# Layer D routed in four chunks of 4, 4, 4 and 3 elements, with places found sooner and indexed rows closer together

## The chip, the cores and the metric

The kernel runs on one core of a Trainium2 chip. The core has five engines that work side by side, each through its own queue in order: TensorE (PE: matrix multiplications, with its weight loads shown as PEld), VectorE (DVE), ScalarE (ACT), GpSimd (POOL) and SyncE (SP, which here only starts transfers). The transfers run on 16 DMA engines. The metric is the device time of one execution in microseconds (us); lower is better.

## The reference

The input is 16 batch elements of 256 tokens with 128 channels, in float32. Four sublayers follow each other, each added to its input after a layer norm: attention a (8 heads, causal, with a term from the geometry of the heads), a mixture of experts, attention b (16 heads, no mask), and the same mixture of experts again with the same weights:

```python
x = x + attn_a(layernorm(x))
x = x + ffn(layernorm(x))
x = x + attn_b(layernorm(x))
x = x + ffn(layernorm(x))

def ffn(tgt):                       # E = 8 experts, F = 512
    logits = einsum('bsd,ed->bse', tgt, Wr) + br
    top_v, top_i = top_k(logits, 2)
    top_w = softmax(top_v)
    router_w = sum(one_hot(top_i, 8) * top_w[..., None], axis=-2)
    h = relu(einsum('bsd,efd->bsef', tgt, W1) + b1)
    o = einsum('bsef,edf->bsed', h, W2) + b2
    return layer_norm(tgt + einsum('bsed,bse->bsd', o, router_w), gamma, beta)
```

Each token uses two of eight experts. What an element needs is its own tokens alone, so elements can be at different sublayers at a time.

## The kernel before

**Work by element and by chunk.** The two attentions run element by element (`attention`), element 0 to 15 of a, then of b. Attention b takes its 16 heads in eight pairs; a pair is scores on PE (tag `s`, L487), row maxima on DVE (L510), then, when all maxima are there, transposed scores (tag `st`, L564), exponentials on ACT, and a weighted sum on PE (L613). The experts run by chunks of elements (`experts`): layer "B" behind attention a, layer "D" behind attention b. `CHUNKS` lists how many elements each chunk has. In D the first five chunks are sorted by expert; the last one, of a single element, is computed with every expert (`every_expert`, called dense), with weights of 0 where a token didn't choose one.

**A sorted chunk.** For each of its elements: a layer norm into the tile `tgt`, its transpose, the router's logits. Then a chain of some 35 small DVE operations with two groups of matmuls between them (`count`, L1005, and `ranks`, L1015 to L1023): the two best experts of each token, each token's rank within its expert, the places of its two rows in the sorted order (`idx`, L1077), and the expert of each tile (`dti`). POOL then writes the rows of `tgt` to those places in memory, 128 rows by one indexed transfer (`scatter`, L1113): two to each 128 tokens, so four to an element. A tile is 128 sorted rows of one expert; since each expert's rows are filled up to whole tiles, a chunk of n elements gets `tiles_of(2n)` = 4n + 7 of them, used or not. Four tiles' rows are read back in one transfer (`rows`) and transposed on PE (`turn_rows`, L1169). Each tile needs its expert's weights (578 KB, SP's queue, ring `we` of six), the first product (`up`, L1182: eight matmul instructions, as each float32 product is two), a ReLU on ACT and DVE, the second product (`down`, L1206, eight more), and a store of four tiles' rows (`os`). When all of a chunk's stores have landed, each element gets its two rows per token back (`gather`, L1271, four indexed transfers on POOL), weighs and adds them on DVE (`part`, L1296) and finishes with the second layer norm (`finish`) and, in D, the write of the output.

**What sets the order.** At build time a planner in Python orders all instructions. Each piece of work is a `Task` with an engine, a planned duration, a `key` (smaller goes first), the tasks that it comes after, and the ring slots (`RINGS`) that it takes and gives back. Keys count pairs of heads: an element of b takes eight, `ends[b]` is its attention's end in this count. The routing chain has the key `key8`, the scatters `key + 0.3`, tile i of a D chunk `key + LATE + PACE_D * i`. While attention still has `st` tasks to place, two `up` tasks are put at least `RATES` apart in planned us (D: 4.1). Indexed transfers are put at least `GAP` = 2.6 planned us apart, and each is made to wait for an ACT instruction that the plan ends between the one transfer (plus 1.3 us) and the next (`apart`). The planned times only set the order within each engine's queue (and these waits); on the chip each engine takes its queue as data comes.

Of the kernel before, what the change touches and what calls it, by code (L numbers as in the profile page):

```python
# [25 lines left out]
NF = F // P  # L26


CHUNKS = {"B": (2, 4, 5, 5), "D": (4, 4, 3, 2, 2, 1)}
CTM = NT * max(max(c) for c in CHUNKS.values())  # L30
TB = 4
NR = 3
# [11 lines left out]

LAT = dict(mem=3.0, qk=6.0, sh=2.4, sc=4.0, rows=4.0, we=4.5, os=5.5, g=5.0)

EARLY = 2.0


WIDE = 6  # L50

RATES = {"B": (4.1, 3.4, 4.1), "D": (4.1,)}


def tiles_of(ct):
# [16 lines left out]
def block_kernel(  # L72
# [20 lines left out]
    NBE = x.shape[0] // T  # L93
    assert all(sum(c) == NBE for c in CHUNKS.values()) and CHUNKS["D"][-1] == 1

# [39 lines left out]
    for b in range(4, 8):  # L135
# [4 lines left out]
    rows_max = [max(  # L140
        tiles_of(NT * n) for c in CHUNKS.values() for k, n in enumerate(c) if k % NX == i
    ) * P for i in range(NX)]
# [80 lines left out]
    def clear_k(i):  # L223
# [11 lines left out]

    RINGS = dict(
        mm=4, att=2, mv=8, lnr=8, nm=6, xn=2, xT2=3, qks=2, mem=3, m=7, ms=2, pT=6, avs=4,
        on=2, oT=2, tgt=14, rl=2, rw=5, didx=5, dti=3, we=6, x4=3, xT=2, hT=3, o4=2,
        r0=NR, r1=NR, y=4, gw=1, ye=1, z=2,
    )  # L240

# [1 line left out]
    GAP = 2.6  # L243
# [118 lines left out]
    all_s, all_st = [], []  # L362

    def attention(kind, b, slot):
# [12 lines left out]
        x = xb[b]  # L377
        ahead = slot - (0.0 if causal else EARLY)
        g = {}
# [344 lines left out]
    order = {"last": None, "xs": {}, "os": {}, "n": 0}  # L724

    def experts(layer, c, ends, need, dense=False):


        n = f"{layer}{c}"
        b0, nb = sum(CHUNKS[layer][:c]), CHUNKS[layer][c]  # L730
        bs = range(b0, b0 + nb)
# [8 lines left out]
        rl_h, tgt_h, t_tgt, t_lg, tT_of = Hold("rl"), {}, {}, [], {}  # L740

        for b in bs:
            key = ends[b] + 0.2
            t0 = (b - b0) * NT

            def tgt_tile(b=b):
                g["tgt", b] = work.tile(
                    [P, NT, C], F32, tag="tgt", name=f"tgt_{n}_{b}", bufs=RINGS["tgt"]
                )
                return g["tgt", b]  # L750
            t_tgt[b], tgt_h[b] = normed(
                lambda b=b: xb[b], f"{n}_{b}", key, [at_x[b]], "tgt", tgt_tile)

            def bias(b=b):

                nc.gpsimd.tensor_tensor(
                    xb[b], xb[b], beta_sb.unsqueeze(1).to_broadcast([P, NT, C]), ALU.add
                )
            at_x[b] = Task("POOL", 0.73, bias, key + 3, [t_tgt[b]])
            t_tT, tT, tT_h = turned(  # L760
                lambda b=b: g["tgt", b], f"{n}_{b}", key, [t_tgt[b]], [tgt_h[b]])
            tT_of[b] = tT, t_tT, tT_h
            mm = Hold("mm")

            def logits(b=b, tT=tT):
                g["lg", b] = ps = ps_mm.tile([P, NT, E], F32, tag="mm", name=f"lg_{n}_{b}")
                for t in range(NT):
                    nc.tensor.matmul(
                        ps[:, t, :], lhsT=tT()[:, t * P:(t + 1) * P], rhs=wr_sb,
                        start=True, stop=True,  # L770
                    )

            def keep_logits(b=b, t0=t0):
                if b == b0:
                    g["rl"] = small.tile([P, ct, E], F32, tag="rl", name=f"rl_{n}",
                                         bufs=RINGS["rl"])
                nc.vector.tensor_tensor(
                    g["rl"][:, t0:t0 + NT, :], g["lg", b],
                    br_sb.unsqueeze(1).to_broadcast([P, NT, E]), ALU.add,
                )  # L780
            e = Task("PE", 0.26, logits, key, [t_tT], take=[mm], use=[tT_h])
            t_lg.append(Task("DVE", 0.1, keep_logits, key, [e] + t_lg[-1:], use=[mm],
                             take=[rl_h] if b == b0 else []))
# [120 lines left out]


        key = max(ends[b] for b in bs) + 0.2
        key8 = key
        k8 = ct * E
        per = 0.14 + 0.0011 * k8
        shape = [P, ct, E]  # L910
# [119 lines left out]
        e = Task("PE", 0.3, count, key8, chain, take=[mm1])  # L1030
        chain = [e]
        dve(0.27, total, use=[mm1])
        e = Task("PE", 0.6, ranks, key8, chain, take=[mm2])
# [77 lines left out]
        def scatter(t, k):  # L1111
            b = b0 + t // NT
            i = apart(nc.gpsimd.indirect_dma_start(  # L1113
                out=x_rows[0:ne * P, :], out_offset=bass.IndirectOffsetOnAxis(
                    ap=g["idx"][:, k, t:t + 1], axis=0),
                in_=g["tgt", b][:, t % NT, :], in_offset=None,
                bounds_check=ne * P - 1, oob_is_err=False,
            ))

            gr = f"sc_{n}"  # L1120
            tc.declare_no_dep(i.ins, group=gr, reason="each row is written once")
            tc.add_to_no_dep_group(gr, i.ins)
        t_sc = []
        free = order["xs"].get(q, []) + zeroed[q]
        for k in range(2):
            for t in range(ct):
                b = b0 + t // NT
                t_sc.append(Task(
                    "POOL", 1.25, lambda t=t, k=k: scatter(t, k), key + 0.3 + 0.01 * len(t_sc),
                    [t_idx[k]] + free, use=[idx_h, tgt_h[b]], kb=64, lat=LAT["sc"] - 1.3,  # L1130
                ))

# [92 lines left out]
        for i in range(ne):  # L1225
            b, j = divmod(i, TB)
            kk = tile_key(i)
            w_h, hT_h, mm1, mm2 = Hold("we"), Hold("hT"), Hold("mm"), Hold("mm")
            if j == 0:
                x4_h, xT_h, mm3, o4_h = Hold("x4"), Hold("xT"), Hold("mm"), Hold("o4")  # L1230
                e = Task("SP", 0.4, lambda b=b: rows(b), kk - 2.5, t_sc, take=[x4_h],
                         kb=256, lat=LAT["rows"])
                t_rows.append(e)
                e = Task("PE", 0.46, lambda b=b: turn_rows(b), kk - 1, [e],
                         take=[mm3, xT_h], use=[x4_h])
                t_xT = Task("ACT", 0.48, lambda b=b: keep_rows(b), kk - 1, [e], use=[mm3])
                t_out = []
            t_load = Task("SP", 0.95 if j == 0 else 0.5, lambda i=i: load(i), kk - 3,
                          [t_ti], take=[w_h], use=[ti_h], kb=592, lat=LAT["we"], order=[t_load])
            t_up_last = t_up = Task("PE", 0.98, lambda i=i: up(i), kk, [t_load, t_xT],  # L1240
                                    take=[mm1, hT_h], use=[w_h, xT_h], order=[t_up_last],
                                    kind="up")
            t_up.rate = RATES[layer][min(c, len(RATES[layer]) - 1)]
            r1 = Task("DVE", 0.27, lambda i=i: relu_v(i), kk, [t_up], use=[mm1, w_h])
            r2 = Task("ACT", 0.76, lambda i=i: relu_s(i), kk, [t_up], use=[mm1, w_h])
            t_dn = Task("PE", 0.98, lambda i=i: down(i), kk, [r1, r2],
                        take=[mm2, o4_h] if j == 0 else [mm2], use=[hT_h, w_h],
                        order=t_dns[-1:])
            t_dns.append(t_dn)
            t_out.append(Task("DVE", 0.2, lambda i=i: keep_out(i), kk, [t_dn], use=[mm2, w_h]))  # L1250
            loads.append(t_load)
            if j == TB - 1 or i == ne - 1:
                stores.append((i, Task(
                    "SP", 0.4, lambda b=b: store(b), kk, t_out + order["os"].get(q, []),
                    use=[o4_h], kb=256, lat=LAT["os"], lag=LAG_OS)))
# [22 lines left out]
        for b in bs:  # L1278
# [3 lines left out]
            for k in range(2):  # L1282
                r_h = Hold(f"r{k}")
                e = [None]
# [52 lines left out]
    ends = {"B": {}, "D": {}}  # L1337
    for kind, b in seq:
        layer = "B" if kind == "a" else "D"
        ends[layer][b] = attention(kind, b, slots[kind, b])  # L1340
        b0 = 0
        for c, k in enumerate(CHUNKS[layer]):
            if b == b0 + k - 1:
                experts(layer, c, ends[layer], slots["b", b0] - NEED if layer == "B" else None,
                        layer == "D" and c == len(CHUNKS[layer]) - 1)
            b0 += k
# [7 lines left out]
    begun = [0.0, 0]  # L1354
    moved = [-GAP]
# [11 lines left out]
    def start(t):  # L1367
        s = max(t.ready + t.lag, free[t.eng])
        if t.eng == "POOL" and t.kb:
            s = max(s, moved[0] + GAP)  # L1370
        if t.kind == "up" and len(all_st) > begun[1]:
            s = max(s, begun[0] + t.rate)
        for h in t.take:
            q, n = rings[h.ring], RINGS[h.ring]
            if len(q) >= n:
                if q[-n].left:
                    return None
                s = max(s, q[-n].done)
            if h.ring == "att" and len(q) > 1:
                if q[-1].left or q[-2].left:  # L1380
                    return None
                s = max(s, q[-1].done, q[-2].done)
        return s
# [34 lines left out]
    while left:  # L1418
        best = None
        for e in ENGS:  # L1420
# [4 lines left out]
            s, t = min(((s, t) for s, t in c if s <= s0), key=lambda st: st[1].key - stay(st[1]))  # L1425
# [3 lines left out]
        s, t, c = best  # L1429
# [94 lines left out]
```

## Time and profile before

The median of three runs is 945.51 us (942.85 to 948.49). The profiled execution took 950.31 us; its span, from the first to the last instruction, is 948.6 us at a mean granted TensorE clock of 0.978.

How the chunks of layer D lie in that span, in us from its start (the element's end is the add at L718; places are the two `idx` casts; the others are starts of the first and last instruction):

| chunk | elements | tiles | last element's end | places | scatters | up-matmuls | gathers |
|---|---|---|---|---|---|---|---|
| 0 | 0-3 | 23 | 441.6 | 470, 471 | 491-531 | 550.2-653.7 | 666-744 |
| 1 | 4-7 | 23 | 577.0 | 608, 611 | 610-650 | 663.4-770.8 | 794-839 |
| 2 | 8-10 | 19 | 677.5 | 706, 708 | 708-739 | 775.4-843.1 | 863-889 |
| 3 | 11, 12 | 15 | 751.7 | 775, 775 | 776-793 | 845.8-877.4 | 892-910 |
| 4 | 13, 14 | 15 | 812.1 | 841, 844 | 842-860 | 878.7-908.9 | 922-939 |
| dense | 15 | - | 851.4 | - | - | 910-934 | - |

The table shows three stretches: attention b with the tiles of B beside it (to 547), attention b with the tiles of D beside it, and from about 850 a tail of tiles alone, closed by the dense element. Element 11 ends at 720.8.

| engine | busy us | share of the span |
|---|---|---|
| DMA, queue of SP (163.69 MB) | | 58.4% of 16 engines |
| DMA, queue of POOL (16.27 MB) | | 5.5% of 16 engines |
| L510 DVE maxima x128 | 155.8 | 16% |
| L1182 PE up, layer D x760 | 102.4 | 11% |
| L1206 PE down, layer D x760 | 107.1 | 11% |
| L1113 POOL scatters, layer D x60 | 60.1 | 6% |
| L1271 POOL gathers, layer D x60 | 62.8 | 7% |

Matmuls are pipelined, so their busy time is the time in which at least one of the group is under way. A view of a stage gives busy times of all engines in a stretch of the span; the chain of waits follows the work that ended last back from the end.

### The profile page before, as it was taken

The numbers are of one execution on the slowest core, as the hardware profiler recorded it, in microseconds if no ns is written. First come the engines' busy times: TensorE is split into PE (matmuls) and PEld (weight loads), VectorE is DVE, ScalarE is ACT, GpSimd is POOL, SyncE is SP. The second block draws the span as 40 slices with busy tenths as digits, with TensorE's granted clock in tenths as the row PEclk, the third lists the DMA queues.
The fourth block names the chain that finished last, engine by engine and source line by source line (L and its number), as shares of the span: only waits on it lengthen the run. The fifth ranks groups of instructions, "written<-read, shape, count | busy, mean of one in ns | idle before, by whom it ended". The sixth has DMA issues, their size and how long they took to land. (4 is left out here: it accounts for less than half of the span.)

```text
span 948.6 us, 24346 instructions
## 1 busy us (share of the span) xinstructions
PE 889.4 (94%) x8941; PEld 720.4 (76%) x8941; DVE 618.1 (65%) x1919; ACT 512.6 (54%) x1188; POOL 416.9 (44%) x553
## 2 busy tenths in 40 slices
PE   7788899998999999999999999999989999899995
PEld 5555688887887778787777777777767877799985
DVE  4578687778657757456686457745766665564666
ACT  5355565665555664565655555556645655545421
POOL 4134635654653554313554225443534314444633
PEclk9799899999999999999999999999999999999998
DMA  4222667666765587575776767566856675599991
GB/s 128 57 70 73 232 194 208 202 208 194 232 187 186 165 207 183 187 204 176 186 197 192 221 180 202 168 190 208 188 142 192 216 185 166 170 306 348 372 316 36
DMA packets 115191, 181.96 MB, mean 192 GB/s; under 512 B 11904, under 2 KB 79360, under 8 KB 115072
## 3 DMA queue, kind: packets, MB, share of 16 engines
q1 hardware_dynamic: 106704, 163.69, 58.4%
q0 software_dynamic: 7936, 16.27, 5.5%
q8 instruction: 71, 1.16, 0.5%
q10 hardware_dynamic: 432, 0.45, 0.2%
q14 instruction: 48, 0.39, 0.1%
HBM read 145.63 MB, written 34.34 MB: 190 GB/s over the span
## 5 line engine op out<-in xcount | busy, mean ns | idle before, releaser
L510 DVE TENSOR_REDUCE m_b<-s_b 128x4 f32<-128x1024 f32 x128 | 155.8, 1220 | 59.9 <-PE s_b L487 39.5
L252 ACT ACTIVATE pT_b<-st_b 128x1024 f32<-128x1024 f32 x128 | 129.9, 1026 | 68.4 <-PE st_b L564 49.2
L252 ACT ACTIVATE hT_D<-h_D,we_D 128x128 f32<-128x128 f32 (+1 forms) x301 | 89.7, 372 | 103.2 <-issue 34.5
L487 PE MATMUL s_b<-qk 31*128 31x256 f32 x1024 | 134.9, 405 | 4.7 <-DVE m_b L510 3.1
L564 PE MATMUL st_b<-qk 32*128 32x256 f32 x1024 | 131.4, 409 | 3.7 <-issue 1.7
L252 ACT ACTIVATE hT_B<-h_B,we_B 128x128 f32<-128x128 f32 x276 | 81.1, 365 | 75.0 <-DVE hT_B L1189 38.6
L1206 PEld LDWEIGHTS o_D<-we_D,hT_D 128*128 128x128 f32 x760 | 93.6, 192 | 23.6 <-ACT hT_D L252 12.0
L1206 PE MATMUL o_D<-we_D,hT_D 128*128 128x128 f32 x760 | 107.1, 287 | 4.5 <-ACT hT_D L252 2.6
L1206 PE MATMUL o_B<-we_B,hT_B 128*128 128x128 f32 x736 | 106.3, 288 | 3.4 <-ACT hT_B L252 2.8
L1206 PEld LDWEIGHTS o_B<-we_B,hT_B 128*128 128x128 f32 x736 | 90.7, 192 | 24.4 <-ACT hT_B L252 14.2
L1182 PE MATMUL h_D<-xT_D,we_D 128*128 128x128 f32 x760 | 102.4, 282 | 0.1
L1271 POOL DMA_INDIRECT r_B<-os,idx_B x64 | 67.9, 1062 | 75.7 <-DMA we_B<-in_we_dram 21.0
L1182 PE MATMUL h_B<-xT_B,we_B 128*128 128x128 f32 x736 | 100.6, 280 | 0.2 <-ACT xT_B L252 0.2
L1182 PEld LDWEIGHTS h_D<-xT_D,we_D 128*128 128x128 f32 x760 | 92.5, 193 | 9.9 <-issue 7.4
L1113 POOL DMA_INDIRECT xs<-tgt_D,idx_D x60 | 60.1, 1001 | 87.7 <-DVE idx_D L1077 17.9
L1182 PEld LDWEIGHTS h_B<-xT_B,we_B 128*128 128x128 f32 x736 | 89.7, 192 | 10.3 <-issue 8.6
L487 PEld LDWEIGHTS s_b<-qk 31*128 31x128 f32 x1024 | 80.8, 186 | 17.7 <-issue 5.5
L564 PEld LDWEIGHTS st_b<-qk 32*128 32x128 f32 x1024 | 79.1, 188 | 17.2 <-issue 7.2
L1271 POOL DMA_INDIRECT r_D<-os,idx_D x60 | 62.8, 1047 | 62.0 <-ACT hT_D L252 30.4
L1113 POOL DMA_INDIRECT xs<-tgt_B,idx_B x64 | 64.7, 1011 | 50.7 <-ACT hT_B L252 12.8
L500 DVE TENSOR_TENSOR s_a<-s_a,cmask 128x512 f32<-128x512 f32 x64 | 44.6, 697 | 42.7 <-PE s_a L487 22.5
L1189 DVE TENSOR_SCALAR hT_D<-h_D,we_D 128x128 f32<-128x128 f32 x95 | 33.0, 350 | 56.7 <-PE h_D L1182 23.7
(401 smaller groups left out, 1620.0 us busy)
## 6 DMA issues: line engine op xcount, KB each, us to landing
we_D<-in_we_dram SPq DMA_DIRECT2D x103, 578.0 KB
we_B<-in_we_dram SPq DMA_DIRECT2D x92, 578.0 KB
qk<-qkm SPq DMA_DIRECT2D x104, 64.0 KB
x_B<-xs SPq DMA_DIRECT2D x20, 256.0 KB
os<-o_B SPq DMA_DIRECT2D x20, 256.0 KB
x_D<-xs SPq DMA_DIRECT2D x20, 256.0 KB
os<-o_D SPq DMA_DIRECT2D x20, 256.0 KB
qkm<-qks_b SPq DMA_DIRECT2D x16, 256.0 KB
```

Source lines behind the costliest of these rows:

```text
L252: i = getattr(nc.scalar, name)(*args, **kw)
L487: nc.tensor.matmul(ps[:, j, col:col + nk], lhsT=qT[r:r + 31, t * P:(t + 1) * P], rhs=kT[r:r + 31, 0:nk], start=True, stop=True,)
L500: nc.vector.tensor_tensor(dg, dg, cmask.unsqueeze(1).unsqueeze(1).to_broadcast([P, 2, 2, P]), ALU.add,)
L510: nc.vector.tensor_reduce(m[:, :, heads].rearrange("p t j -> p j t"), ps.rearrange("p j (t k) -> p j t k", k=T), axis=AX.X, op=ALU.max, ne ...
L564: nc.tensor.matmul(ps[:, j, col:col + T - q0], lhsT=kT[r:r + 32, t * P:(t + 1) * P], rhs=qT[r:r + 32, q0:T], start=True, stop=True,)
L1113: i = apart(nc.gpsimd.indirect_dma_start(out=x_rows[0:ne * P, :], out_offset=bass.IndirectOffsetOnAxis(ap=g["idx"][:, k, t:t + 1], axis=0) ...
L1182: nc.tensor.matmul(ps[:, f, :], lhsT=w[:, f * P:(f + 1) * P], rhs=g["xT", b][:, j * P:(j + 1) * P], start=True, stop=True,)
L1189: nc.vector.tensor_scalar(g["hT", i][:, f, :], g["h", i][:, f, :], g["w", i][:, W_B1 + f:W_B1 + f + 1], 0.0, ALU.add, ALU.max)
L1206: nc.tensor.matmul(ps, lhsT=g["hT", i][:, f, :], rhs=g["w", i][:, W_2 + f * C:W_2 + (f + 1) * C], start=(f == 0), stop=(f == NF - 1),)
L1271: apart(nc.gpsimd.indirect_dma_start(out=g["r", k, b][:, t, :], out_offset=None, in_=o_rows[0:ne * P, :], in_offset=bass.IndirectOffsetOnAxis(
```

## The change

- Layer D's sorted chunks are 4, 4, 4 and 3 elements, in place of 4, 4, 3, 2 and 2. The dense element stays. Layer B's chunks stay.
- `AHEAD` holds three numbers that are taken off keys: of the elements' layer norms and logits (0), of the routing chain (6, in both layers), and of the scatters (0).
- Two `up` tasks of D are planned 4.1 us apart in the first two chunks and 4.4 in the other two.
- The ring of `tgt` tiles has 18 slots, where it had 14.
- `turn_rows` of one batch of tiles is never put ahead of that of the batch before, across chunks as well.
- Indexed transfers are planned 2.6 us apart as before while more than 24 `st` tasks are still to be placed (three elements of attention b), and 1.4 behind that. With 1.4 no ACT instruction lies between two that follow at that distance, so `apart` names none.

```diff
-CHUNKS = {"B": (2, 4, 5, 5), "D": (4, 4, 3, 2, 2, 1)}
+CHUNKS = {"B": (2, 4, 5, 5), "D": (4, 4, 4, 3, 1)}
...
+AHEAD = 0, 6, 0
...
-RATES = {"B": (4.1, 3.4, 4.1), "D": (4.1,)}
+RATES = {"B": (4.1, 3.4, 4.1), "D": (4.1, 4.1, 4.4, 4.4)}
...
-        on=2, oT=2, tgt=14, rl=2, rw=5, didx=5, dti=3, we=6, x4=3, xT=2, hT=3, o4=2,
+        on=2, oT=2, tgt=18, rl=2, rw=5, didx=5, dti=3, we=6, x4=3, xT=2, hT=3, o4=2,
...
-            key = ends[b] + 0.2
+            key = ends[b] + 0.2 - AHEAD[0]
...
         key = max(ends[b] for b in bs) + 0.2
-        key8 = key
+        key8 = key - AHEAD[1]
...
-                    "POOL", 1.25, lambda t=t, k=k: scatter(t, k), key + 0.3 + 0.01 * len(t_sc),
+                    "POOL", 1.25, lambda t=t, k=k: scatter(t, k), key + 0.3 - AHEAD[2] + 0.01 * len(t_sc),
...
                 e = Task("PE", 0.46, lambda b=b: turn_rows(b), kk - 1, [e],
-                         take=[mm3, xT_h], use=[x4_h])
+                         take=[mm3, xT_h], use=[x4_h], order=[order.get("turn")])
+                order["turn"] = e
...
         if t.eng == "POOL" and t.kb:
-            s = max(s, moved[0] + GAP)
+            s = max(s, moved[0] + (GAP if len(all_st) > begun[1] + 24 else 1.4))
```

## The prediction

> **What bounds the kernel now.** I read the busy times and the slices first. TensorE (PE) is busy nearly all the time; the last slices also show the DMA engines full.
>
> ```profile
> PE 889.4 (94%) x8941; PEld 720.4 (76%) x8941; DVE 618.1 (65%) x1919; ACT 512.6 (54%) x1188; POOL 416.9 (44%) x553
> ...
> PE   7788899998999999999999999999989999899995
> ...
> DMA  4222667666765587575776767566856675599991
> GB/s 128 57 70 73 232 194 208 202 208 194 232 187 186 165 207 183 187 204 176 186 197 192 221 180 202 168 190 208 188 142 192 216 185 166 170 306 348 372 316 36
> ```
>
> Then busy time by stage, all engines (columns: stretch, length, busy us and instructions of PE, weight load, DVE, ACT, POOL, granted clock, DMA share, GB/s).
>
> ```profile
> 680.00:700.00 20.00, 17.20 (x175) 12.94 (x174) 14.38 (x46) 9.68 (x20) 8.96 (x12) 0.91 0.68 169
> ...
> 820.00:840.00 20.00, 20.00 (x197) 16.95 (x200) 12.15 (x54) 11.67 (x29) 9.78 (x12) 1.00 0.67 211
> 840.00:860.00 20.00, 19.89 (x188) 18.66 (x177) 10.87 (x47) 10.62 (x34) 9.14 (x12) 1.00 0.99 328
> 860.00:880.00 20.00, 19.49 (x167) 18.89 (x167) 10.65 (x49) 9.17 (x31) 10.04 (x11) 1.00 1.02 366
> 880.00:900.00 20.00, 19.90 (x169) 19.22 (x168) 13.44 (x55) 10.24 (x35) 12.67 (x15) 1.00 1.02 369
> ```
>
> The reader is to see that PE has no idle time worth the name behind 820, with attention over and only expert tiles left. So PE work taken out of layer D comes off the end, as long as the tail never runs out of tiles.
>
> The same view for the up-matmuls alone (L1182, tile h_D) has 232 of them in 840 to 900, eight to a tile: 29 tiles in 60 us, **2.07 us of span for a tile** with its share of all else.
>
> Third, what delays a chunk's rows: DVE and PE in order of time for the last chunk (elements 13, 14), then POOL's scatters.
>
> ```profile
> 826.91 0.27 DVE L1010 COPY dtot_D<-dt_D 32x128 f32<-32x128 f32 x1
> ...
> 839.55 0.19 DVE L1029 COPY drk_D<-dr_D 128x40 f32<-128x40 f32 x1
> ...
> 841.41 0.17 DVE L1077 CAST idx_D<-dsf_D 128x4 int32<-128x4 f32 x1
> ```
> ```profile
> 838.40 0.40 PE L1015 MATMUL dr_D<-cst_sb,dtot_D 32*128 32x32 f32 x2
> ```
> ```profile
> 842.35 1.02 POOL L1113 DMA_INDIRECT xs<-tgt_D,idx_D  x1 [1.96 <-ACT avs_b L252]
> 844.95 0.99 POOL L1113 DMA_INDIRECT xs<-tgt_D,idx_D  x1 [1.57 <-ACT hT_D L252]
> 846.25 0.98 POOL L1113 DMA_INDIRECT xs<-tgt_D,idx_D  x1 [0.31 <-issue]
> ...
> 859.94 0.99 POOL L1113 DMA_INDIRECT xs<-tgt_D,idx_D  x1 [1.24 <-ACT xT_D L252]
> ```
>
> Two delays: `ranks` is ready at 827.2 and stands 11 us in PE's queue behind expert tiles; and eight scatters take 17.6 us, 2.51 apart, held back by the ACT instructions that `apart` names, though two can follow each other in 1.30 (844.95, 846.25). That chunk's first tile starts at 878.7, behind a backlog, so now it costs nothing.
>
> Last, the chain that ended last: dense expert matmuls from 909.97 to 939.0, then two finishes.
>
> ```profile
> 900.66 6.34 DMA r_D<-os,idx_D
> ...
> 935.40 3.58 PE o_D L869 x32
> ...
> 944.77 0.35 DVE x L804
> ```
>
> **The change, part by part.** The sum is made in the profiled execution (span 948.6, its time 950.31; the median of the runs, 945.51, is 4.8 lower).
>
> (a) *Chunks of D.* A chunk of n elements has 4n + 7 tiles: 23+23+19+15+15 = 95 now, 23+23+23+19 = 88 after. Seven go: 7 x 2.07 = **-14.5**. Bounds: bare matmuls in the chain cost 0.89 + 0.95 (0.89 for h_D x8, 1.90 for o_D x16), -12.9; the whole-run busy times (102.4 + 107.1) / 95 = 2.2 give -15.4. Were the DMA engines the tail's bound instead, seven tiles of 578 KB weights and 128 KB rows at 366 GB/s would still be 13.8 us, so both bounds give it back. Scatters and gathers stay 60 and 60.
>
> (b) *One routing round fewer.* PE loses dt (0.41) and dr (about 1.0): **-1.4**, ends 0 and -1.6. Its 35 or so DVE steps of 0.2 us lie beside PE.
>
> (c) *Places six pairs sooner* (both layers, eight chains). The chain, `count` and `ranks` go ahead of maxima and tiles that now stand before them. Gain: chunk 1's first tile (663.4, its predecessor's last 653.7) comes sooner, and PE's gaps in 640 to 720 are 6.1 us. Loss: a maxima reduce behind a chain holds back scores; PE's one long wait of that kind is 2.52 us, at 690.77. I take **-1**, ends -4 and +4: most of that wait came from a gather that DVE stood behind, not from the chain.
>
> (d) *Chunk 2 comes an element later* (last element 11, done 720.8, in place of 10, done 677.5). Places: 9 us to the first router maximum (677.5 to 686.5), then 12 us of chain unhindered (last chunk: 4.1 + 2.4 + 1 + 4.1), so 742; 16 scatters at 1.4 end at 765; from last scatter to first tile took 13 us (650 to 663): 778. Chunk 1's last tile starts at 770.8, so PE has attention alone for some 5 us; without tiles it lost 14% of 680 to 700 (17.20 of 20). With a half-clock spell, which that window's clock of 0.91 shows (3.4 us at half, 1.7 lost), **+2**; ends 0 and +4.5.
>
> (e) *Start of the tail.* Chunk 3 (elements 12 to 14) is found after 812.1, as the last chunk is now, but has 12 scatters and a smaller backlog ahead. First router maximum 820.4, unhindered chain 832, 11 x 1.4 + 1 = 849, and 9 us to the tile (859.9 to the transposed rows at 868.8): 858. From 820 to 860 PE ran 15 tiles (120 up-matmuls), so 9 us of other work. Up to 858 it wants 38 - 9 = 29 us of tiles, 14. Of chunk 2, at a real 4.7 us each (4.4 planned; 4.1 planned ran at 4.4), 9 have run by 820 and 14 are left. It just fits: **+2** for a tile's error. The other end: ranks wait as now (idx at 843.7) and scatters stay 2.51 apart (27.6 + 1), first tile at 881, 23 us of idle PE: +23.
>
> (f) *The end.* The last chunk has 12 gathers where it had 8, and its three finishes. They started 5 us behind the last store and ran 921.6 to 938.7 under 29 us of dense matmuls. At 1.4 apart, with two 1 us powers between, twelve need 17.4, as eight did; **+2** for POOL's other work. If spacing stays 17.0 / 7 = 2.43, 11 x 2.43 = 26.7, +9.6.
>
> (g) *Rows closer together* also in gathers: DVE stands in its queue for late ones (2.82 us at 904.3, PE idle 1.01 behind it). I take two such, **+2**, ends 0 and +6.
>
> (h) The slower pace of tiles (4.4) moves work from attention to tail and is counted in (e). Larger tgt ring, order on `turn_rows`: 0, they take no engine time; cover for an ordered transpose is the six weight slots loaded ahead.
>
> Sum: -14.5 - 1.4 - 1 + 2 + 2 + 2 + 2 = -8.9. 950.3 - 8.9 = 941.4 in such an execution, **936.6 for the median**.
>
> [...] At (g) the row is the gather at 900.66, 6.34 us to land with the DMA engines full. [...] At (e) the row is the clock of 0.91 in 680 to 700. [...] The row shows the fall already with gaps of 2.5 us.
>
> **Rivals.** *Rows closer, end later.* The last gathers do not close up and land late: (f) 9.6 and (g) 6 give +2.7, 948.2, no measurable change. For: DMA share 1.02, ACT-paced waits now. Against: DMA share falls to 0.26 in 920 to 940, and 1.30 us between scatters is seen.
>
> *The tail runs dry* (slower side). PE waits for chunk 3's rows: (c) 0, (d) 4.5, (e) 23 give -14.5 - 1.4 + 4.5 + 23 + 2 + 2 = +15.6, 961. For: the 11 us that `ranks` stood in PE's queue, and 12 scatters in place of 8. Against: ranks goes ahead by six pairs, the scatters need no ACT. With the other terms as forecast it decides the sign from 11 us of idle on, when the first tile of chunk 3 comes later than 869 on the old scale.
>
> *It doesn't do what it says:* the planner places the sooner chain where it was, because logits, not priority, hold it; then (c) is 0, and (e) goes from the places at 843.7: 16.4 of scatters at 1.4 and 9 to the tile make 869, 11 us of idle. -14.5 - 1.4 + 2 + 11 + 2 + 2 = +1.1, 946.6, no change.
>
> **How the numbers follow.** A change under 0.5% (4.7 us) can't be told from none. Forecast 0.70, own range 928 to 942 (by ends of a, c, d and part of e); gathers 0.10; dry tail 0.12; no sooner places 0.08. Faster (below 940.8): 0.70 and the lower part of two rivals, less the forecast's top: 0.71. Same 0.17. Slower 0.12. Range 927 to 950: it takes in both no-change rivals and leaves out the dry tail and a little below.
>
> **What would show it.** 704 up-matmuls at L1182; scatters of the last D chunk under 1.6 us apart; `ranks` within 3 us of `dtot`; PE over 19 of 20 us in each window from attention's end to the dense experts; dense matmuls ending 12 to 15 us sooner; the last finish within 7 us of them. Wrong would be: a PE hole over 5 us between attention and the last chunk's first tile, or the last gather starting after the dense matmuls.

## The result and the profile after

The changed kernel takes **977.99 us** (median of 4 runs, 974.51 to 979.64) beside 946.43 for the kernel before on the same chip (942.85 to 948.49): a ratio of **1.0333**, 95% interval 1.0288 to 1.0377. The forecast was 936.6 with a range of 927 to 950, so sign and range were both wrong. Times here are medians of all executions, while each ratio compares the fast executions alone (an execution counts as slow when it is over 1.5% above its kernel's fastest), so it need not be the quotient of two medians. The profiled execution took 976.97 us, with a span of 975.2 at a mean granted clock of 0.963, against 948.6 and 0.978 before. Line numbers of the kernel after, and of runs made from it, are 2 or 3 higher than those of before (L1182 becomes L1184, L1271 becomes L1274).

The page's busy times and slices of the kernel after:

```profile
PE 887.4 (91%) x8814; PEld 713.8 (73%) x8814; DVE 607.6 (62%) x1872; ACT 507.9 (52%) x1164; POOL 416.0 (43%) x553
...
PE   7788899999999999999999999999997889877994
...
PEclk9799899999999999999999999999999899977896
DMA  4122766666676767676766856576665546666861
```

There are 127 matmul instructions fewer, 112 of them the up- and down-matmuls of seven tiles (704 of each, as forecast), but PE's busy time falls by 2.0 us only. The loss begins in the 31st slice (from 731 us on): PE is at 7 to 9 tenths, its clock at 7 to 9 and the DMA row at 4 to 8 up to the last slice but one, where before it stood at 9 for four slices from the 36th on.

Busy time by stage (stretch, length, busy us and instructions of PE, weight load, DVE, ACT, POOL, granted clock, DMA share, GB/s):

```profile
740.00:760.00 20.00, 12.69 (x121) 10.71 (x118) 7.73 (x23) 9.23 (x24) 13.52 (x15) 0.97 0.52 152
...
800.00:820.00 20.00, 16.25 (x162) 11.57 (x161) 12.47 (x48) 9.80 (x20) 11.11 (x15) 1.00 0.47 136
820.00:840.00 20.00, 19.60 (x191) 16.67 (x188) 12.24 (x53) 13.64 (x33) 3.48 (x6) 1.00 0.69 206
840.00:860.00 20.00, 13.48 (x94) 10.32 (x93) 4.03 (x21) 4.05 (x13) 11.81 (x12) 0.78 0.48 157
860.00:880.00 20.00, 15.82 (x111) 14.92 (x109) 7.22 (x30) 6.29 (x21) 1.67 (x3) 0.84 0.89 277
880.00:900.00 20.00, 16.62 (x116) 15.68 (x115) 5.31 (x23) 6.71 (x21) 9.64 (x10) 0.84 0.61 203
```

In 740 to 760 and 840 to 860, where PE loses most, *all* other engines but POOL are low too, and so are the DMA engines (in 800 to 820 it is ACT and the DMA engines, not DVE). POOL is busy there, with indexed transfers. A hole in which PE waits for rows looks different: in that of e13, below, the DMA engines are at 0.90 in its first half (854.5 to 860) and at 0.60 in the second. In 820 to 840, with 3.48 us of POOL, PE is full.

An account by PE up to its last matmul (964.6 after, 939.0 before): idle time 77.2 against 49.6 (+27.6), busy -2.0, together +25.6; from there to the end 10.6 against 9.6. Of the idle time 34.9 us lie behind 730, against 5.2. Seven tiles and a routing round were priced at 15.9 us of PE, so behind the -2.0 some 14 us of other busy time came in. The clock makes 8.3 of it (half of what PE works at a granted clock of 0.50, 51.8 us against 35.1): behind 730 it costs 14.7 more (32.8 us at half rate, 3.4 before), ahead of 730 it happened to cost 6.4 less. What the other 5.6 us are isn't shown.

The order of time for the last chunk. First DVE (start, length, line):

```profile
834.31 0.28 DVE L1012 COPY dtot_D<-dt_D 48x128 f32<-48x128 f32 x1
836.41 0.22 DVE L1031 COPY drk_D<-dr_D 128x56 f32<-128x56 f32 x1 [0.72 <-PE dr_D L1025]
...
840.10 0.17 DVE L1079 CAST idx_D<-dsf_D 128x6 int32<-128x6 f32 x1
```

The forecast's sign for the sooner places is there: `ranks` follows `dtot` in 2.1 us (12.6 before). Then POOL's scatters, twelve from 841.06 on, 1.28 apart:

```profile
841.06 1.09 POOL L1115 DMA_INDIRECT xs<-tgt_D,idx_D  x1 [14.42 <-DVE dsf_D L1075]
842.45 0.99 POOL L1115 DMA_INDIRECT xs<-tgt_D,idx_D  x1 [0.31 <-issue]
...
855.25 0.97 POOL L1115 DMA_INDIRECT xs<-tgt_D,idx_D  x1 [0.30 <-issue]
```

And under them PE, which has the previous chunk's tiles to do, then ACT and DVE:

```profile
846.77 0.38 PE L615 MATMUL av_b<-pT_b,v 128*32 128x256 f32 x1 [0.79 <-issue]
847.07 0.71 PE L1208 MATMUL o_D<-we_D,hT_D 128*128 128x128 f32 x4
848.21 0.70 PE L1208 MATMUL o_D<-we_D,hT_D 128*128 128x128 f32 x4 [0.42 <-issue]
849.63 0.98 PE L1184 MATMUL h_D<-xT_D,we_D 128*128 128x128 f32 x4 [0.73 <-issue]
851.06 1.08 PE L1184 MATMUL h_D<-xT_D,we_D 128*128 128x128 f32 x3 [0.45 <-issue]
852.50 1.28 PE L1184 MATMUL h_D<-xT_D,we_D 128*128 128x128 f32 x4 [0.36 <-issue]
```
```profile
858.20 0.59 ACT L254 COPY avs_b<-av_b 128x512 f32<-128x512 f32 x1 [11.64 <-PE h_D L1184]
```
```profile
858.29 0.29 DVE L1216 TENSOR_TENSOR o_D<-o_D,we_D 128x128 f32<-128x128 f32 x1 [14.24 <-PE h_D L1184]
```

This is the shape to remember. (A *release* is the raising of the semaphore that another engine waits for.) From the fifth scatter on PE goes forward about four matmuls at a time, at first one group every 1.43 us (848.21, 849.63, 851.06, 852.50), and before each group it "waits for nothing that the profile shows" (`issue`). ACT has stood 11.64 us and DVE 14.24, both for PE, although PE instructions that release them ended at 847.14, 848.91, 853.07 and 857.30. In the trace's records PE's semaphore is raised at 846.05, then not until 858.17, then four times in 0.28 us. The *releases* came late, in a bundle, 2.9 us after the last scatter began. In 850 to 858 DVE and ACT are at 0.00 and the DMA engines at a share of 0.16 (before, in the same stretch: 4.01 and 3.62 us, and 0.98); the weight transfers on SP's queue wait with the rest, one of them 14.7 us for DVE's `o_D`. The same steps of 1.43 us stand under the gathers of 794 to 802 (PE goes on at 799.89, 801.33, 802.77, 804.18), and a PE gap of 5.9 us under the scatters of 747 to 758.

The chain that ended last closes as before, dense expert matmuls and then finishes on DVE (start, length, line):

```profile
951.61 3.57 PE o_D L871 x32
955.18 2.30 PE h_D L850 x8
...
971.43 0.35 DVE x L806
```

### The profile page after: what moved, and what is told of

It reads as the page before. It is cut to its first block, busy times and chain, and to the rows that moved or that the text cites. A ratio compares the mean times of both kernels' runs of the same rounds, so it can differ in the third digit from the quotient of the medians.

```text
span 975.2 us, 23953 instructions
## 1 busy us (share of the span) xinstructions
PE 887.4 (91%) x8814; PEld 713.8 (73%) x8814; DVE 607.6 (62%) x1872; ACT 507.9 (52%) x1164; POOL 416.0 (43%) x553
## 4 chain that ended last, share of the span: by engine, by line
PE 64%; DVE 10%; DMA 6%; ACT 6%; issue 5%; POOL 1%; SPq 1%; ACTq 0%; POOLq 0%; DVEq 0%
PE h_D L1184 8%; PE o_D L1208 7%; PE o_B L1208 7%; PE h_B L1184 6%; PE s_b L489 6%; PE av_b L615 6%; PE st_b L566 5%; DVE m_b L512 2%; PE s_a L489 2%; PE st_a L566 2%; PE av_a L615 2%; PE h_D L850 1%; PE o_D L871 1%; DVE m_a L507 1%; PE pj_b L426 1%
## 5 line engine op out<-in xcount | busy, mean ns | idle before, releaser
L489 PE MATMUL s_b<-qk 31*128 31x256 f32 x1024 | 138.9, 401 | 3.3 <-ACT pT_b L254 2.1
L254 ACT ACTIVATE hT_D<-h_D,we_D 128x128 f32<-128x128 f32 (+1 forms) x280 | 84.6, 374 | 109.8 <-DVE hT_D L1191 49.8
L566 PE MATMUL st_b<-qk 32*128 32x256 f32 x1024 | 135.3, 401 | 2.1 <-DVE m_b L512 0.8
L1208 PE MATMUL o_D<-we_D,hT_D 128*128 128x128 f32 x704 | 103.0, 294 | 11.3 <-issue 6.6
L1208 PEld LDWEIGHTS o_D<-we_D,hT_D 128*128 128x128 f32 x704 | 90.1, 200 | 30.0 <-ACT hT_D L254 13.7
L1184 PE MATMUL h_D<-xT_D,we_D 128*128 128x128 f32 x704 | 102.4, 293 | 8.5 <-issue 6.7
L1274 POOL DMA_INDIRECT r_D<-os,idx_D x60 | 62.8, 1047 | 105.1 <-ACT hT_D L254 37.5
L1184 PEld LDWEIGHTS h_D<-xT_D,we_D 128*128 128x128 f32 x704 | 91.2, 203 | 22.0 <-issue 18.0
L1184 PE MATMUL h_B<-xT_B,we_B 128*128 128x128 f32 x736 | 100.9, 280 | 0.6 <-ACT v L254 0.4
L1274 POOL DMA_INDIRECT r_B<-os,idx_B x64 | 67.5, 1055 | 76.1 <-ACT ms_b L254 21.2
L1184 PEld LDWEIGHTS h_B<-xT_B,we_B 128*128 128x128 f32 x736 | 90.5, 193 | 9.0 <-issue 7.0
L489 PEld LDWEIGHTS s_b<-qk 31*128 31x128 f32 x1024 | 82.7, 184 | 15.9 <-ACT pT_b L254 5.3
L566 PEld LDWEIGHTS st_b<-qk 32*128 32x128 f32 x1024 | 81.2, 184 | 15.6 <-issue 4.2
L1115 POOL DMA_INDIRECT xs<-tgt_D,idx_D x60 | 59.9, 999 | 72.9 <-ACT pT_b L254 19.6
L1191 DVE TENSOR_SCALAR hT_D<-h_D,we_D 128x128 f32<-128x128 f32 x88 | 30.5, 349 | 75.0 <-PE h_D L1184 36.4
```

The costliest lines, as they stand in the source:

```text
L254: i = getattr(nc.scalar, name)(*args, **kw)
L489: nc.tensor.matmul(ps[:, j, col:col + nk], lhsT=qT[r:r + 31, t * P:(t + 1) * P], rhs=kT[r:r + 31, 0:nk], start=True, stop=True,)
L566: nc.tensor.matmul(ps[:, j, col:col + T - q0], lhsT=kT[r:r + 32, t * P:(t + 1) * P], rhs=qT[r:r + 32, q0:T], start=True, stop=True,)
L1115: i = apart(nc.gpsimd.indirect_dma_start(out=x_rows[0:ne * P, :], out_offset=bass.IndirectOffsetOnAxis(ap=g["idx"][:, k, t:t + 1], axis=0) ...
L1184: nc.tensor.matmul(ps[:, f, :], lhsT=w[:, f * P:(f + 1) * P], rhs=g["xT", b][:, j * P:(j + 1) * P], start=True, stop=True,)
L1191: nc.vector.tensor_scalar(g["hT", i][:, f, :], g["h", i][:, f, :], g["w", i][:, W_B1 + f:W_B1 + f + 1], 0.0, ALU.add, ALU.max)
```

## The experiments

The theory at this point: *indexed transfers close behind each other hold up the other engines' releases*. The rivals: the last chunk's rows are late for another reason (chunk sizes, the tail that runs dry), or the sooner routing chain does harm. In each diff "after" or "before" names the kernel that it starts from.

**One part alone, or one undone.** e1 is after with transfers 2.6 us apart and tied to ACT all the way. e2 is before with the close rule alone. e3 is after, 1.4 apart in the plan, but each transfer waits for the last ACT instruction that the plan ends since the one before. e4 is before with the new chunks and the `tgt` ring alone.

```diff
 # e1, from after
-            s = max(s, moved[0] + (GAP if len(all_st) > begun[1] + 24 else 1.4))
+            s = max(s, moved[0] + GAP)
 # e2, from before
-            s = max(s, moved[0] + GAP)
+            s = max(s, moved[0] + (GAP if len(all_st) > begun[1] + 24 else 1.4))
 # e3, from after
-                since = [i for done, i in marks if moved[0] + 1.3 <= done <= s - 0.1]
+                since = [i for done, i in marks if moved[0] + (1.3 if len(all_st) > begun[1] + 24 else 0.0) <= done <= s - 0.1]
 # e4, from before
+CHUNKS = {"B": (2, 4, 5, 5), "D": (4, 4, 4, 3, 1)}
...
+        on=2, oT=2, tgt=18, rl=2, rw=5, didx=5, dti=3, we=6, x4=3, xT=2, hT=3, o4=2,
```

> The whole change, but indexed transfers stay 2.6 planned us apart to the end, each with its ACT instruction to wait for. Burst theory (transfers on POOL that follow each other at 1.28 us hold up the other engines): the holes of PE at 740-760, 800-820 and 840-860 go, the half-clock spells after 730 fall from 37 us to under 10, time 930 to 942. Dry-tail rival (the larger chunks come too late whatever the spacing): the last chunk's rows come later still, time 960 or more. Rival that the last chunk's 12 gathers set the end: 945 to 955 with the last gather behind the dense matmuls.

> The kernel before with the closer spacing alone. Burst theory: PE stops in steps of 1.4 us under each run of scatters or gathers behind some 745, idle of PE behind 730 goes from 5 to 25 us or more, time 965 to 990. Dry-tail rival: nothing to lose here, since the backlog of tiles stays, time 940 to 950.

> The whole change with 1.4 planned us between indexed transfers, but each near the end again waits for the last ACT instruction that the plan ends between it and the one before. If the missing wait is what hurts (POOL runs ahead of the other engines in bursts at 1.28): time 930 to 945, transfers spread by what ACT does. If 1.4 us is too close by itself: 960 to 985, with the same holes.

> The kernel before with the chunks 4, 4, 4, 3, 1 (and the 18 slots that they need) alone. Burst theory and my forecast's sum: seven tiles fewer, some wait for the last chunk's rows since places and scatters come as late as before, 935 to 950. Dry-tail rival at its full price: 955 to 965, with 15 to 25 us of idle PE ahead of the last chunk's first tile.

| run | us | ratio to before | 95% |
|---|---|---|---|
| e1 apart again | 943.05 | 1.0123 | 1.0093 to 1.0153 |
| e2 close alone | 932.21 | 1.0029 | 1.0001 to 1.0057 |
| e3 close, tied | 927.79 | 0.9969 | 0.9943 to 0.9995 |
| e4 chunks alone | 939.17 | 1.0079 | 1.0052 to 1.0105 |

These ran on another chip, on which the kernel *before* takes 930.26, not 946. By them the theory seems dead: e2 has the close transfers and loses 0.3%, and with the spacing put back (e1) the kernel is slower than without. In e1 the tail does run dry (PE, start and length, with the idle time before it in brackets):

```profile
841.97 0.61 PE L770 MATMUL lg_D<-wr_sb,xT_D 128*128 128x8 f32 x4 [0.46 <-ACT xT_D L254]
853.15 2.01 PE L1171 MATMUL xt_D<-ident,x_D 128*128 128x128 f32 x8 [10.57 <-DMA x_D<-xs]
```

Here the releaser is a named transfer, the last chunk's rows: places at 823, scatters 822 to 846, first transposed rows at 853. e4 has such a hole of 11.6 us. So the dry tail is real, but most of it is what *spaced* transfers bring.

**The whole change on such a chip, and its parts there.** e5 is after itself. e6 is e3 with `AHEAD = 0, 0, 0`. e7 is after with a wait for the plan's last ACT instruction before every fourth close transfer.

```diff
 # e7, from after, in the stretch where transfers may be close
+                    turns[0] += 1
+                    since = [i for done, i in marks if moved[0] <= done <= s - 0.1] * (turns[0] % 4 == 0)
```

> The changed kernel itself, beside the others on one chip. If its holes come from indexed transfers without a wait: ratio to before 1.02 to 1.04 again, PE in steps of 1.43 us under the last chunk's scatters. If they belong to the chip on which it was first run: ratio 0.99 to 1.005, like the tied version (0.997).

> The tied version (ratio 0.997) with the routing chain's key as before. If sooner places are worth what my sum says (1 us and a tail that just fits): 2 to 10 us slower than tied, ratio 0.999 to 1.008. If the ranks stand in PE's queue by the plan anyway: ratio 0.992 to 1.000.

> The changed kernel with a wait on the plan's last ACT instruction before every fourth of the indexed transfers near the end. If what hurts is POOL far ahead of the other engines, a wait in four is enough: ratio 0.995 to 1.005. If it needs only three or four transfers in a row without a wait: ratio 1.015 or more.

Beside 930.94 for before: e5 929.14, ratio 0.9974 (0.9946 to 1.0003); e6 936.09, 1.0051 (1.0021 to 1.0081); e7 930.38, 0.9971 (0.9932 to 1.0009). **The same kernel that lost 3.3% loses nothing here.** Two later runs of it say the same (e9 1.001, e18 1.0001), as does the tied kernel's (e10 0.999). Sooner places are worth 0.6 to 0.8%, some 6 to 7 us: e6, without them, is that much above e7 and e5 (and e3 by its ratio), and its PE idle time behind 730 is 18.3 us against 9.0 in e3.

**Smaller last chunk.** If the dry tail is the chunks' price, a last sorted chunk of two elements behind a bigger backlog should take it away and keep the 88 tiles. e8 is e3 with chunks of 5, 4, 4, 2; e9 is after, e10 is e3 again.

```diff
+CHUNKS = {"B": (2, 4, 5, 5), "D": (5, 4, 4, 2, 1)}
...
+    rows_max = [max(tiles_of(NT * n) for c in CHUNKS.values() for n in c) * P] * NX
```

> The tied version with the same 88 tiles cut as 5, 4, 4, 2, 1 elements (all three buffers of sorted rows as large as the largest chunk). The last chunk is of two elements again: 8 scatters and 8 gathers, and its rows should be there about 5 us sooner. If what eats the seven tiles is the wait for the last chunk (idle PE, the half-clock spell behind it, 12 gathers at the end): idle behind 730 from 9 to under 5, ratio 0.980 to 0.992. If the first chunk of five comes too late instead, PE misses tiles around 550: ratio 0.997 or more.

> The changed kernel once more. On a chip like the first one (before at 946): ratio 1.02 to 1.04 with PE in steps under the runs of transfers. On a chip like the other two (before at 930): 0.994 to 1.002.

> The tied version once more, beside it. If the chip is like the first one and the missing waits are what it punishes: ratio 0.995 to 1.010 where the changed kernel has 1.02 or more. If waits that are satisfied early don't matter there either: within 0.004 of the changed kernel. On a chip like the other two: 0.993 to 1.001.

Beside 928.32: e8 919.31 (four executions, 910.89 to 926.2), ratio 0.9888 (0.9784 to 0.9993); e9 929.11, 1.001 (0.998 to 1.004); e10 927.75, 0.999 (0.9958 to 1.0023). The tail of e8, by stage:

```profile
820.00:840.00 20.00, 18.82 (x167) 18.44 (x167) 12.35 (x56) 10.38 (x34) 12.38 (x15) 1.00 1.03 356
840.00:860.00 20.00, 19.77 (x171) 19.22 (x170) 9.54 (x38) 9.41 (x32) 4.81 (x6) 1.00 1.02 361
```

and that of e9, by stage and by PE's order of time:

```profile
840.00:860.00 20.00, 16.04 (x119) 15.25 (x120) 7.19 (x34) 7.82 (x24) 7.32 (x9) 0.83 0.80 255
```
```profile
842.09 0.86 PE L351 MATMUL tp_D<-ident,tgt_D 128*128 128x128 f32 x2 [2.83 <-ACT tgt_D L254]
...
845.85 1.94 PE L1171 MATMUL xt_D<-ident,x_D 128*128 128x128 f32 x8 [1.41 <-DMA x_D<-xs]
```

e8 has full PE, full clock and full DMA engines where e9 has a small hole and 6.8 us at half clock. So seven tiles less do pay, once the rows of the last chunk are there in time. In e9 against e2 (spans 928.1 and 928.0) one sees how they are given back: PE busy -11.3 (864.7 against 876.0; without the time at half clock it is -16.5), idle +10.0 (51.6 against 41.6, of that 5.9 behind 730), the end +1.3.

**Back on the first kind of chip.** e11 is after again, e12 is e3 again.

> The changed kernel again, to meet a chip like the first one. There (before near 946): 970 to 985, PE in steps of 1.43 us under the scatters of the last two chunks. Else 925 to 935.

> The tied version beside it. On a chip like the first one: 935 to 955 if the missing waits are what it punishes, 965 or more if the closeness or the chunks are. Else 922 to 932.

Beside 946.64 for before: e11 980.92, ratio 1.0356 (1.0281 to 1.0431); e12 965.3, 1.0191 (1.0091 to 1.029), two executions of each. So it goes with the chip and isn't chance: where before takes 946 to 947 the change costs 3.3 to 3.6%, where before takes 928 to 931 it costs nothing that can be told. In e12 the waits leave up to seven transfers in a row (after: up to twelve), and half of the loss stays.

**The two theories on that kind.** e13 is e1 again, e14 is e2 again, e15 is e1 with e8's chunks.

> The change with 2.6 planned us and the wait on ACT between all indexed transfers, on another chip. On a chip like the first one (before near 946): ratio 1.008 to 1.016 as on the other kind if runs of transfers are what that chip punishes, 1.03 or more if it is anything else of the change. On the other kind: 1.010 to 1.015.

> The kernel before with the closer spacing alone. On a chip like the first one: ratio 1.015 to 1.04, with PE in steps of 1.43 us under scatters and gathers from the fifth of a run on, if the runs do it; 0.998 to 1.006 if it takes the change's larger chunks. On the other kind: 1.000 to 1.006.

> The 88 tiles as 5, 4, 4, 2, 1 elements with places sooner and 2.6 planned us between indexed transfers. With the last chunk small the spacing should matter little: ratio 0.985 to 0.997 on either kind of chip, which would beat both kernels where the runs of transfers can't hurt. If the chunk of five or its 17.6 us of scatters leaves PE without tiles: 1.000 or more.

| run, beside 946.9 | us | ratio | 95% |
|---|---|---|---|
| e13 apart again | 954.61 | 1.0073 | 1.0024 to 1.0122 |
| e14 close alone | 981.72 | **1.0375** | 1.0308 to 1.0442 |
| e15 5, 4, 4, 2, apart | 946.01 | 0.9959 | 0.9908 to 1.001 |

The table is from eight executions of e13, three of e14 and nine of e15. This settles which part of the change does it. e14 has the old chunks, the old backlog and the old routing chain; one line of spacing costs 34.8 us. Its stages and, under the gathers, PE:

```profile
780.00:800.00 20.00, 13.10 (x100) 10.07 (x96) 7.05 (x22) 5.42 (x11) 7.12 (x9) 0.74 0.38 119
...
880.00:900.00 20.00, 13.49 (x91) 12.61 (x90) 3.14 (x11) 5.94 (x20) 12.38 (x13) 0.73 0.85 265
```
```profile
811.50 0.65 PE L613 MATMUL av_b<-pT_b,v 128*32 128x256 f32 x4 [0.78 <-issue]
812.93 0.59 PE L613 MATMUL av_b<-pT_b,v 128*32 128x256 f32 x2 [0.79 <-issue]
```

The same kernel on the second kind of chip (e2), where the transfers follow each other no slower:

```profile
760.00:780.00 20.00, 19.35 (x218) 14.95 (x210) 13.59 (x34) 11.89 (x24) 15.22 (x17) 1.00 0.63 188
780.00:800.00 20.00, 19.61 (x200) 15.92 (x196) 15.02 (x61) 12.71 (x28) 13.95 (x18) 1.00 0.70 207
```
```profile
775.59 1.00 POOL L1271 DMA_INDIRECT r_D<-os,idx_D  x1 [0.30 <-issue]
...
778.19 1.00 POOL L1271 DMA_INDIRECT r_D<-os,idx_D  x1 [0.30 <-issue]
```

1.30 us apart, and PE at 19.4 and 19.6 of 20. On the first kind PE's groups of a few matmuls every 1.43 us are back (811.50, 812.93), in attention's own matmuls (L613) as well, which read no sorted rows. One sum sets the profiles apart, that of PE's gaps with `issue` ahead behind 700 us: 19.1 us in after, 20.6 in e11, 14.0 in e14 and 7.2 in e12; 2.2 in before, 0.2 in e13 and 1.1 in e15, whose transfers are spaced, on the same kind of chip; 0.0 in e2, e3, e5, e9 and e18, close on the other kind.

e13 is the change without its close transfers, and the tail runs dry as in e1:

```profile
853.93 0.61 PE L770 MATMUL lg_D<-wr_sb,xT_D 128*128 128x8 f32 x4 [0.46 <-ACT xT_D L254]
865.44 1.94 PE L1171 MATMUL xt_D<-ident,x_D 128*128 128x128 f32 x8 [10.90 <-DMA x_D<-xs]
```

Against the profile of before its PE is busy 18.2 us less (871.2 against 889.4) and idle 14.9 more (64.5 against 49.6, 10.9 of it this hole), and from the last matmul to the end it takes 16.9 us in place of 9.6: -18.2 + 14.9 + 7.3 = +4.0, the difference of the spans, 952.6 and 948.6. e15, with a last chunk of two, has no such hole and cannot be told from before.

**How long may a run be?** e16 is after with 2.6 us and an ACT wait behind every third close transfer, e17 the same with 5, 4, 4, 2, e18 is after.

```diff
 # e16, from after
+            s = max(s, moved[0] + (GAP if len(all_st) > begun[1] + 24 or turns[0] % 3 == 0 else 1.4))
...
+                turns[0] = turns[0] + 1 if s < moved[0] + 2.5 else 1
```

> The changed kernel, but behind every third indexed transfer near the end the next is planned 2.6 us later and waits for ACT. On a chip of the first kind (before near 946): ratio 1.000 to 1.010 and no steps of PE if runs of three are harmless there; 1.02 or more if any close pair hurts. On the second kind: 0.997 to 1.006.

> The same with the chunks 5, 4, 4, 2, 1. First kind: ratio 0.980 to 0.996, faster than before. Second kind: 0.985 to 0.993, like the tied version of this cut.

> The changed kernel beside them. First kind: ratio 1.030 to 1.040; second kind: 0.995 to 1.002.

Beside 930.17: e16 931.16, ratio 1.0006 (0.9972 to 1.004); e17 922.16, 0.9897 (0.9833 to 0.9961); e18 930.58, 1.0001 (0.9963 to 1.0038). Before's 930 shows that these met a chip of the second kind, where runs of any length cost nothing, so the question is not answered. They confirm e8: chunks of 5, 4, 4, 2 gain about 1% there. No version is shown to beat both kernels on both kinds; e8 and e17 were not run on the first.

## Why the prediction was wrong, step by step

- **(a), (b) seven tiles and a routing round, -15.9: right.** 704 up-matmuls, and without the time at half clock PE is busy 16.8 us less in e13 than in before, and 16.5 less in e9 than in e2.
- **(g) rows closer together, +2 with ends 0 and +6: the step that failed.** It priced a close transfer as one that may *land late*, from a single DVE stall of 2.82 us. What it costs on this kind of chip is that PE's matmuls are held (5.9 us at most in after), and its releases of ACT and DVE with them (11.0 us late at most): e14 has the close spacing alone and measures +34.8 us (0.3% with e2 on the other kind), and the change with close transfers (+3.3%) is 2.6% above the change with spaced ones (e13, +0.7%). The trace of before had two scatters 1.30 apart, and the forecast read from them that 1.30 can be kept up for twelve. POOL did keep it up. What a run of twelve does to the others was in no row of before, whose longest runs are of four; its cost was bounded by rows that could not contain it.
- **(e) start of the tail, +2 with ends 0 and +23: mis-sized.** With spaced transfers e13 measures 10.9 us of hole and 3.0 us of work at half clock behind it, so 12.4 in all. Close on the second kind e9 has 4.2 of hole (2.83 ended by the dense element's layer norm, 1.41 by the rows) and 5.0 us at half clock, 6.7. The mechanism, PE that has no tiles until chunk 3's rows are there, is that of the dry-tail rival. Of the working, the places at 832 came out (831.8 and 833.9 in e13), though by other steps: element 14 ended at 798.7, where the forecast took 812.1. The 9 us from the last scatter to its rows were misread: the rows copied at 868.7 are the chunk before's (its last batch, of three tiles), while the last chunk's own were first transposed at 873.1, behind a backlog. That the 9 is near what spaced runs need (7.6 in e1, 7.9 in e13, 8.1 in e4) is luck; e9 took 11.6.
- **(c) sooner places, -1: most of their worth stood in (e).** The rival without them is 10.0 us above the forecast (+1.1 against -8.9). On the second kind of chip e6 against e3 says some 7 us, through the tail (PE's idle time behind 730): they bring the last chunk's places forward.
- **(d) chunk 2 later, +2:** not measured alone. e13 has 9.8 us of PE idle time behind 730 besides the hole, before 5.2; a loss of the size forecast fits, but other terms share those 4.6.
- **(f) the end, +2 with +9.6 if spaced: near, both ways.** From the last matmul to the end after takes 10.6 us (+1.0); spaced, e13 takes 16.9 (+7.3).
- **(h) 0:** nothing in the runs speaks against it; it was not run alone.

The forecast's inner fault is that (e) and (f) were only small *because* transfers were close, and closeness was taken as free. On this kind of chip chunks of 4, 4, 4, 3 with spaced transfers lose 0.7%, with close ones 3.3%; neither way leads to -0.9%. Even where closeness is free the change comes out at 0.9974 to 1.001. There the larger (e), 6.7 us, takes back under half of the tiles' 16.5. The rest, by e9 against e2, is 4.1 us of idle PE and 2.8 us of half clock ahead of 730, 1.7 of other idle time behind it and 1.3 at the end; these are single executions, and what causes those parts isn't shown.

**The rivals.** "Rows closer, end later" (948.2) named the right part of the change and the wrong price and place: little at the end (+1.0 us), nearly all in the stretches of transfers. "The tail runs dry" (961) has the right sign, and its mechanism is shown in e1, e4 and e13, but it is not what made 978: e14 has no dry tail and is slower still. "Doesn't do what it says" falls with `ranks` 2.1 us behind `dtot`.

**The landing time and the clock.** On (g) the forecast went by the row of 6.34 us to land; that was not the point, since what e14 lost was not the landing time of single gathers. On the clock: behind e13's hole the granted clock is 0.50 from 854.8 to 868.4, of which PE worked 3.0 us, so 1.5 us are lost. In after the gaps of the steps of 848 to 857 are 0.4 to 1.3 us, and the trace has the clock at 0.50 from 851.1 on, for 13.7 us.

## What to carry to other kernels

A spacing or a wait that looks like a lost chance may keep up something that no row shows; before a term is bounded by the nearest rows, ask whether the trace can contain the case at all, and widen the bound if it can't. In after PE, ACT, DVE and the DMA queues all went low together (850 to 858: 4.26 us of 8, twice 0.00, and a share of 0.16) and PE moved in even steps with `issue` ahead of each; where a profile looks so, look for what POOL issues close behind each other (here every 1.28 us, while PE steps by 1.43) before you look for missing data. Of the fewer, larger chunks tried here those kept their saved padding whose last one was small enough that its rows arrived behind the backlog: 5, 4, 4, 2 (0.9888 and 0.9897 on the second kind, 0.9959 and not told from 1 on the first).

## What the hardware showed

- **Held releases.** Indexed transfers at 1.28 to 1.30 us (0.97 to 1.00 on POOL and 0.30 between), in runs of eight to twelve: PE in groups of two to five matmuls, for the most part every 1.43 us, or stopped for up to 5.9 (6.3 in e11), and releases up to 11.0 us late and then four of them within 0.28 (after: a matmul that ended at 847.14, its release at 858.17). One of after's five such runs, from 943 under dense matmuls, shows no such gap. Shorter runs on the same kind of chip are mixed. The eight runs of three in e13 and the two of four in before have no gap of PE with `issue` above 0.24 us, but the run of four from 733.7 in after has one of 1.75 (1.85 in e11; none at that place in e9, on the other kind). A run of five in e15 has one of 0.83, a run of six under dense matmuls none; e12, with up to seven, has half of the loss. From which length on it counts, whether length alone decides, and what in the chip holds the releases, stays open.
- **Two kinds of chip.** The same kernel before takes 946 to 947 us on at least two chips and 928 to 931 on three others, 1.7% apart. Close transfers make a kernel 3.3 to 3.8% slower than before on the one (after, e11, e14) and -0.3 to +0.3% on the other (e2, e5, e9, e18). Nothing that was read in the profiles names the difference: on both kinds POOL issues the transfers at the same rate, and in e2 and e14 the median packet of a weight transfer takes the same 179 ns.
- **The clock.** Ahead of the last matmul, before and after have the granted clock at 0.50 in spells of 3.4, 6.8, 10.2 and 13.7 us, and in each of the two profiles these start on one grid of 3.41 us (those at 851.1, 878.4 and 898.9 in after are 8 and 6 grid steps apart). In the 3.41 us just ahead of these three PE is busy 1.69, 1.18 and 1.28. Single gaps of PE of 2.5 to 2.8 us stand ahead of such spells too: 2.5 at 691 in before, then 3.4 us at half; 2.83 in e9, then 6.8. Of e13's 13.7 us at half PE worked in 3.0 and stood in the rest.
